# A table of steps for every piece of a chunk, fp8 transposes in the FFN, and a searched order for the end, in a two-layer scan, attention and FFN kernel

## The chip, the cores and the metric

The kernel runs on one core of one Trainium2 chip. Its engines work side by side, each through its own list of instructions in order: TensorE (PE, matmuls and transposes), VectorE (DVE), ScalarE (ACT), GpSimd (POOL) and SyncE (SP, which issues most DMAs). The metric is the device time of one execution in microseconds (us).

## What is computed

The input x is 4 images of 64 x 64 tokens with 96 channels, so 4 batches of 4096 tokens. Layer 0 adds to x a gated linear scan over the tokens of each batch, and layer 1 adds an attention without softmax and then an FFN whose numbers are rounded to fp8 (5 exponent and 2 mantissa bits) and fp16. Cut to what matters:

```python
# layer 0, of x after a group norm, per batch; S = 16 states per channel
proj = layernorm(x) @ W_in            # value, gate, delta (96 each), A, B, C (1536 each)
h_new = d * (A_t * h) + d * (B_t * u_t)      # along the tokens
y = sigmoid(gate) * sum_s(C_t * h_new)
x = x + y @ W_out
# layer 1
q, k, v = split(layernorm(x) @ Wqkv)          # 6 heads
y = (q @ k.T * D ** -0.5) @ v                 # no softmax
x = x + y @ Wff
h = relu(qlinear(layernorm(x), W1, b1))       # q_mul: fp8, q_acc: fp16
x = x + qlinear(h, W2, b2)
```

The attention has no softmax, so it is a matrix per batch: the kernel sums the gram matrix of the normalised tokens over a whole batch, and makes of it one 97 x 96 matrix (`rmat`) by which layer 1 multiplies each token. So layer 1 of a batch can't start before layer 0 of the whole batch has ended.

## The kernel before

**Chunks and steps.** A batch is cut into 8 chunks of 512 tokens, 32 chunks in all. A chunk's scan has 1536 rows (96 channels x 16 states), which are 12 tiles of 128 rows: one tile is one *step*, and there are K = 384 steps. The main loop at the end of the kernel goes through the steps and issues for each the same core work, in this order:

- PE: `b_proj` for the tile three steps on, `a_proj` for the next tile, `c_proj` for this one (three matmuls of 512 columns each);
- ACT: `b_copy` after `b_proj`, `keep` of the last column of h;
- POOL: `b_mul` for the tile two steps on, and, for the tiles whose number mod 12 is in `ON_POOL`, `c_mul_pool` of the tile before;
- DVE: `scan` of this tile (line 767), `a_mul` of the next (line 760), and for tiles not in `ON_POOL` `c_mul` (line 791);
- then `call(s)`: everything that the table `steps` holds for this step; last, `c_copy` on ACT for a tile in `ON_POOL`.

**Pieces of a chunk.** All else is put into `steps` by `at(step, fn)`, relative to the chunk's first step s0. The *front* (lines 696 to 718) makes the chunk's inputs: `load_x`, then `centre` and `scale` (POOL), `stats` (DVE), `rstd` (POOL), `apply` (ACT), `transpose` (PE, into the tile xnt), `affine` and `upper` (ACT), `low` (DVE, then three DMAs), the projections d and u (PE) with `d_out` (ACT) and `du_out` (DVE), `write` and `read` (DMAs which spread d and d*u over 128 partitions through DRAM into `rep`), and the gate. The *gathers* add up the four groups of states by DMA. The *tail* (lines 831 to 921) follows on the scan: `state_sum` (PE, tile y_ps), `gated` (DVE), `project_out` (PE, tile o_ps), `residual` and `stats` (DVE), `rstd` (POOL), `apply` (ACT), `transpose` (PE), `keep`, `spill` (DMA to DRAM), `gram` (PE) and its sum. `ffn` (lines 967 to 1106) is layer 1 of a chunk, 8 chunks later: `fetch` (DMA), `attention` (PE, tile a_ps), `residual`, `stats`, `rstd`, `apply` (ACT), `transpose` (PE, tile xq_ps), `quant_in` (ACT), three `hidden` matmuls (PE, tile h_ps) each with a `relu` of three ACT operations, `project_out` (PE), `round_out` (ACT), `bias_out` and `total` (POOL), `store` (DMA). `group_norm` computes the next batch's group norm.

**PSUM.** The core work has banks of its own (A twice, B, C, D); everything in `steps` takes its bank from one ring M of three, in the order in which it is issued, and so waits until the last reader of the tile three before is done.

**The end.** What would fall behind step 384 isn't put into `steps` but becomes a job of the list scheduler `Plan` (lines 387 to 460), with an engine, a cost, its predecessors and the buffers it takes and frees. `Plan.run` takes again and again the job that can start first; among those within `LOOK` us of it the one of lower rank, then the one with the longest chain behind it. In the end `apply` of layer 1 of batch 3 is on DVE (`apply_vector`), `relu` is on DVE, and `round_out` is on DVE for odd chunks. The first steps are ordered by the same class (`planned_start`).

The numbers that place the pieces before are:

```python
FRONT = -22
SUMS = -28
FFN0 = 28
ON_POOL = (1, 3, 6, 10)
```

Of the kernel before, what the change touches and what calls it, by code (L numbers as in the profile page):

```python
# [37 lines left out]
FRONT = -22  # L38
SUMS = -28
FFN0 = 28  # L40
ON_POOL = (1, 3, 6, 10)
# [4 lines left out]
def conv_attn_hybrid_kernel(  # L46
# [35 lines left out]
        "xn2": 1, "xq": 1, "h16": 1, "hr": 1, "hq": 1, "y16": 1, "yb": 1, "o": 1,  # L82
# [106 lines left out]
    xa_t, xal_t = [], []  # L189
    for r in range(2):  # L190
        t = const.tile([P, J, CA], F32, tag=f"xa{r}", name=f"xa{r}")
        nc.gpsimd.memset(t[:, :, C:CA], 1.0)
        xa_t.append(t)
        t = const.tile([CA, J, P], F32, tag=f"xal{r}", name=f"xal{r}")
        nc.gpsimd.memset(t[C:CA], 1.0)
        xal_t.append(t)

# [12 lines left out]
    w2_sb = sb("xn2", [C, HID], F32, "w2_sb")  # L210
# [125 lines left out]
    class LayerNorm:  # L336
# [32 lines left out]
        def apply(self, dst, src):  # L369
            for j in range(J):  # L370
                nc.scalar.activation(
                    dst[:, j, 0:C], src[:, j, :], AF.Identity,
                    bias=self.nmr[:, j : j + 1], scale=self.r[:, j : j + 1],
                )

        def apply_vector(self, dst, src):
            for j in range(J):
                nc.vector.tensor_scalar(  # L378
                    dst[:, j, 0:C], src[:, j, :], self.mv[:, j, 0:1], self.r[:, j : j + 1],
                    ALU.subtract, ALU.mult,  # L380
                )
# [5 lines left out]
    class Plan:  # L387
        HOP = 0.15
        LOOK = 0.3

# [19 lines left out]
        def run(self, fill=None):  # L410
# [13 lines left out]
            taken, back = self.taken, {}  # L424
            todo = list(self.jobs)
            while todo:
                best = None
                for n, j in enumerate(todo):
                    if any(a["end"] is None for a in j["after"]):
                        continue  # L430
                    t = self.time.get(j["engine"], 0.0)
                    for a in j["after"]:
                        hop = 0.0 if a["engine"] == j["engine"] else self.HOP
                        t = max(t, a["end"] + a["late"] + hop)
                    full = False
                    for b in j["take"]:
                        r = b.split(":")[0]
                        if len(taken[r]) >= self.rings[r]:
                            k = taken[r][-self.rings[r]]
                            full = full or k not in back  # L440
                            t = max(t, back.get(k, 0.0) + self.HOP)
                    if full:
                        continue
                    key = (t, j["rank"], -tail(j), n)
                    if best is None or t < best[0][0] - self.LOOK or (
                        t < best[0][0] + self.LOOK and key[1:] < best[0][1:]
                    ):
                        best = key, j
                (t, _, _, n), j = best
                todo.pop(n)  # L450
# [5 lines left out]
                j["end"] = self.time[e] = t + j["cost"]  # L456
                for b in j["take"]:
                    taken[b.split(":")[0]].append(b)
                for b in j["free"]:
                    back[b] = j["end"] + j["late"]  # L460
# [103 lines left out]
    def group_norm(b, s0):  # L564
# [11 lines left out]
        when = [s0 + SUMS + NT * n for n in range(NCH)]  # L576
# [119 lines left out]
    def front(b, i, s0, f=None):  # L696
        s = s0 + FRONT
        if f is None:
            f = Front(b, i)
            if (b, i) not in xt:  # L700
                at(s - 3, load_x, b, i)
            at(s, f.centre, nc.gpsimd)
            at(s + 1, f.scale, nc.gpsimd)
            at(s + 2, f.stats)
            at(s + 3, f.ln.rstd)
            at(s + 5, f.apply)
            at(s + 7, f.transpose)
            at(s + 8, f.affine)
            at(s + 9, f.upper)
            at(s + 9, f.low)  # L710
            at(s + 12, f.proj, 2)
            at(s + 13, f.d_out)
            at(s + 13, f.proj, 0)
            at(s + 14, f.du_out)
            at(s + 14, f.write)
            at(s + 15, f.read)
        at(s + 20, f.proj, 1)
        at(s + 21, f.gate_out)
# [89 lines left out]
    def state_sum(g, last=None, first=None):  # L808
# [17 lines left out]
        {"A": 2, "B": 1, "C": 1, "M": 3, "xal": 2, "xat": 1, "bu": 5, "h": 3, "rep": 2,  # L826
# [3 lines left out]
    end.last = {}  # L830

    def tail(b, i, s0):


        nm, g = f"{b}_{i}", b * NCH + i
        v, ln = {}, LayerNorm(1e-5, f"a_{nm}")
# [46 lines left out]
        def gram_add():  # L883
            nc.gpsimd.tensor_tensor(grams[b], grams[b], v["add"], ALU.add)

        plan = [
            (5, state_sum, g), (6, gated), (7, project_out), (8, residual), (8, ln.stats, t),
            (9, ln.rstd), (12, ln.apply, xa, t), (14, transpose), (15, keep), (16, spill),
            (21, gram), (22, gram_out),
        ]  # L890
        if i:
            plan.append((23, gram_add))
        for n, fn, *args in plan:
            if s0 + n < K:
                at(s0 + n, fn, *args)
        if s0 + plan[-1][0] < K:
            return
# [3 lines left out]
        job, a = end.job, None  # L901
        if s0 == K:
            for sh, late in ((0, 0.0), (2, 0.0), (3, 2.4)):
                w = job(f"wait{sh}", late, lambda: None)
                a = job("PE", 0.5, state_sum, g, sh, sh > 0, after=[a, w],
                        take=["B:y"] if sh == 0 else [])
            a = job("DVE", 0.7, gated, after=[a], free=["B:y"])
            a = job("PE", 0.5, project_out, after=[a], take=["B:o"])
            a = job("DVE", 0.56, residual, after=[a], free=["B:o"])
            a = job("DVE", 1.1, ln.stats, t, after=[a], take=[f"mv:a{i}"])  # L910
            a = job("POOL", 1.3, ln.rstd, False, after=[a])
        else:
            job("wait", 0.0, lambda: None, take=[f"mv:a{i}"])
        if s0 == K:
            applied = job("DVE", 1.3, ln.apply_vector, xa, t, after=[a], free=[f"mv:a{i}"])
        else:
            applied = job("ACT", 1.55, ln.apply, xa, t, free=[f"mv:a{i}"])
        a = job("PE", 0.4, gram, after=[applied, end.last.get("gram")], take=[f"B:g{i}"])
        end.last["gram"] = job("DVE", 0.25, gram_sum, after=[a], free=[f"B:g{i}"])
        a = job("PE", 0.45, transpose, after=[applied], take=[f"C:a{i}"])  # L920
        a = job("ACT", 0.57, keep, after=[a], free=[f"C:a{i}"], take=[f"xat:{i}"])
        end.last[b, i] = job("SP", 0.5, spill, after=[a], late=2.5, free=[f"xat:{i}"])
# [4 lines left out]
    def attn_matrix(b, s0):  # L927
# [31 lines left out]
        for n, (args, out) in enumerate(chain):  # L959
            if s0 < K:  # L960
                at(s0 + 24 + n, mm, *args)
                at(s0 + 24 + n, out)
            else:
                a = end.job("PE", 0.3, mm, *args, after=[a], take=[f"B:r{n}"])
                a = end.last["r"] = end.job("DVE", 0.25, out, after=[a], free=[f"B:r{n}"])

    def ffn(b, i, s0):
# [6 lines left out]

        def fetch():
            v["xa"] = xal_t[i % 2]
# [12 lines left out]
        def apply():  # L989
            v["xn"] = tile_of("xn2", "bu", [P, J, C], F32, "xn2")  # L990
            (ln.apply_vector if b == B - 1 else ln.apply)(v["xn"], t)

        def transpose():
            ps = v["ps"] = bank("C" if phase["end"] else "M", [C, TC], f"xq_ps_{nm}")
            for j in range(J):
                nc.tensor.transpose(ps[:, j * P : (j + 1) * P], v["xn"][:, j, :], ident)
# [365 lines left out]
```

## Time and profile before

| what | value |
|---|---|
| median of 3 runs | 1214.04 us (1212.67 to 1214.79) |
| the profiled execution | 1214.51 us, span 1212.8 us |
| granted clock of TensorE | 0.989 |
| first scan starts, last scan starts | 30.8 us, 1134.4 us |
| chunks 1 to 9 (layer 0 only), from scan to scan | 299.3 us, 33.3 us each |
| chunks 10 to 30 (with layer 1), from scan to scan | 733.1 us, 34.9 us each |
| rmat of batch 3 is there | 1150.5 us |
| `scan` on DVE | 336 of 1269 ns and 48 of 1210 ns |
| `b_mul` on POOL | 384 of 1496 ns |

The profile's page gives busy time for each engine, first as totals and then in slices. Durations in it overlap on one engine (an operation's end[...] lies behind the start of the next one), so what an operation costs an engine is read from the distance of two starts in the timeline. The list of waits says which engine stood idle, for which instruction, and who released it.

### The profile page before, as it was taken

The page shows a single profiled execution, that of the slowest core. Times are in us where ns is not written, and L with a number is a line of the kernel's source. Part 1 is how long each engine was busy: PE and PEld are TensorE (multiplying, and loading weights), DVE is VectorE, ACT ScalarE, POOL GpSimd, SP SyncE. Part 2 cuts the span into 40 slices and gives each one's busy share as a digit, 9 for nine tenths or more (in the row PEclk, how much of TensorE's full clock was granted, in tenths as well). Part 3 has the DMA queues.
Part 4 walks back from the last instruction along what each step waited for, and adds up shares of the span by engine and source line. Part 5 has one row for each costly group of instructions (what it writes and reads, how often), then busy time and mean ns, then how long its engine had stood idle before and what let it go on. Part 6 is the DMA issues. An engine that isn't in the chain of part 4 may idle for free. (4 is left out here: it accounts for less than half of the span.)

```text
span 1212.8 us, 19189 instructions
## 1 busy us (share of the span) xinstructions
PE 1155.5 (95%) x5888; PEld 872.8 (72%) x5888; DVE 1125.7 (93%) x2103; ACT 809.9 (67%) x1812; POOL 1031.6 (85%) x1171
## 2 busy tenths in 40 slices
PE   6899999999999999999999999999999999999884
PEld 5677777777777777777777777677777777777652
DVE  6799999999999999999999999999999999999794
ACT  4655656655565787777777777777777777776574
POOL 3988878888888888999999888999999899988654
PEclk8999999999999999999999999999999999999998
DMA  7656767677776676677667766766776667666221
GB/s 185 141 133 145 165 151 164 147 161 164 168 160 151 153 166 151 154 168 176 159 151 164 172 154 146 174 154 149 154 174 154 154 158 174 153 145 142 66 66 40
DMA packets 104289, 182.14 MB, mean 150 GB/s; under 512 B 42637, under 2 KB 50769, under 8 KB 104186
## 3 DMA queue, kind: packets, MB, share of 16 engines
q1 hardware_dynamic: 90060, 106.96, 36.5%
q0 software_dynamic: 13536, 73.93, 30.2%
q8 instruction: 47, 0.77, 0.3%
q14 instruction: 56, 0.46, 0.1%
q10 hardware_dynamic: 590, 0.02, 0.0%
HBM read 69.12 MB, written 24.77 MB: 77 GB/s over the span
## 5 line engine op out<-in xcount | busy, mean ns | idle before, releaser
L751 POOL TENSOR_TENSOR bu<-bu,rep 128x512 f32<-128x512 f32 x384 | 557.7, 1496 | 14.7 <-ACT bu L748 9.2
L748 ACT ACTIVATE bu<-Bps,b_bac 128x512 f32<-128x512 f32 x384 | 263.7, 687 | 286.0 <-PE Bps L244 269.0
L767 DVE TENSOR_TENSOR_SCAN h<-Aps,state,bu 128x512 f32<-128x512 f32 x336 | 426.4, 1269 | 13.2 <-POOL bu L751 3.5
L760 DVE SCALAR_TENSOR_TENSOR Aps<-Aps,b_bac,rep 128x512 f32<-128x512 f32 x384 | 282.5, 736 | 25.1 <-PE Aps L244 24.6
L244 PE MATMUL Bps<-xs,w 128*128 128x512 f32 x768 | 268.1, 430 | 3.7 <-ACT bu L748 3.4
L244 PE MATMUL Aps<-xs,w 128*128 128x512 f32 x768 | 249.6, 406 | 14.2 <-DVE h L767 13.3
L800 POOL TENSOR_TENSOR ch<-ch,h 128x512 f32<-128x512 f32 x128 | 193.5, 1512 | 2.6 <-ACT ch L797 2.4
L244 PEld LDWEIGHTS Aps<-xs,w 128*128 128x128 f32 x768 | 138.6, 189 | 70.5 <-DVE h L767 42.3
L244 PEld LDWEIGHTS Bps<-xs,w 128*128 128x128 f32 x768 | 129.4, 191 | 46.5 <-issue 24.3
L244 PE MATMUL Aps<-xl,w 128*128 128x512 f32 x384 | 152.6, 397 | 0.3 <-DMA w<-w 0.3
L244 PE MATMUL Bps<-xl,w 128*128 128x512 f32 x384 | 151.8, 395 | 0.0
L244 PE MATMUL Dps<-xs,w 128*128 128x512 f32 x384 | 121.1, 397 | 0.0
L244 PE MATMUL Cps<-xs,w 128*128 128x512 f32 x384 | 120.8, 395 | 0.0
L806 POOL DMA_DIRECT2D ch<-ch x94 | 89.0, 947 | 15.1 <-DMA ch<-ch 11.5
L791 DVE SCALAR_TENSOR_TENSOR ch<-Dps,b_bac,h 128x512 f32<-128x512 f32 x128 | 94.7, 740 | 0.5 <-PE Dps L244 0.4
L791 DVE SCALAR_TENSOR_TENSOR ch<-Cps,b_bac,h 128x512 f32<-128x512 f32 x128 | 95.0, 742 | 0.0
L244 PEld LDWEIGHTS Aps<-xl,w 128*128 128x128 f32 x384 | 72.4, 188 | 18.4 <-DMA w<-w 1.0
L244 PEld LDWEIGHTS Bps<-xl,w 128*128 128x128 f32 x384 | 72.5, 189 | 17.5
L244 PEld LDWEIGHTS Dps<-xs,w 128*128 128x128 f32 x384 | 72.4, 189 | 17.5
L244 PEld LDWEIGHTS Cps<-xs,w 128*128 128x128 f32 x384 | 72.3, 188 | 17.5
L244 PE MATMUL Dps<-xl,w 128*128 128x512 f32 x192 | 76.0, 396 | 0.0
L244 PE MATMUL Cps<-xl,w 128*128 128x512 f32 x192 | 75.7, 394 | 0.0
(196 smaller groups left out, 2056.0 us busy)
## 6 DMA issues: line engine op xcount, KB each, us to landing
ch<-ch POOLq DMA_DIRECT2D x94, 768.0 KB, 6.5
rep<-ddd SPq DMA_DIRECT2D x124, 384.0 KB, 6.4
ddd<-dd SPq DMA_DIRECT2D x31, 384.0 KB, 3.0
xl<-lo SPq DMA_DIRECT2D x62, 128.0 KB, 2.4
x<-in_x_dram SPq DMA_DIRECT2D x32, 192.0 KB, 2.9
xatd<-xat SPq DMA_DIRECT2D x32, 192.0 KB, 3.1
xal<-xatd SPq DMA_DIRECT2D x32, 192.0 KB, 5.8
out_dram<-o SPq DMA_DIRECT2D x32, 192.0 KB, 2.1
```

The lines of the kernel that those rows point to most:

```text
L244: nc.tensor.matmul(ps, lhsT=wt[:, n], rhs=mv, start=(n == 0), stop=(n == 2))
L748: nc.scalar.activation(self.bu, self.b_ps, AF.Identity, bias=self.bias(0))
L751: nc.gpsimd.tensor_tensor(self.bu, self.bu, rep[self.b, self.i][:, 1, self.cg], ALU.mult)
L760: nc.vector.scalar_tensor_tensor(self.a_ps, self.a_ps, self.bias(1), rep[self.b, self.i][:, 0, self.cg], ALU.add, ALU.mult,)
L767: nc.vector.tensor_tensor_scan(self.h, self.a_ps, self.bu, 0.0 if self.i == 0 else state[self.sh, self.cg], ALU.mult, ALU.add,)
L791: nc.vector.scalar_tensor_tensor(self.slot(), self.c_ps, self.bias(2), self.h, ALU.add, ALU.mult)
L800: nc.gpsimd.tensor_tensor(self.ch, self.ch, self.h, ALU.mult)
L806: nc.gpsimd.dma_start(chs[g, 0], chs.pop((g, sh)), accum_op=ALU.add)
```

## The change

1. The numbers for the pieces of front, gathers, tail and `ffn` become one table `AT` of steps relative to s0 (for `ffn` relative to the step 96 after its chunk's s0), with other values. x is loaded at -28 and centred at -15, 13 steps later, where it was loaded at -25 and centred at -22. `ON_POOL` is (1, 2, 7, 10).
2. In `ffn` the normalised tokens are written as fp8 into one of two constant tiles of 128 columns (`xn8`, zeros in the last 32), and the transposes are fp8 matmuls with an fp8 identity.
3. A group of pieces (such as `transpose`, `keep` and `spill`) either lies wholly before step 384, or wholly in the end (`place`). The jobs of the end follow from that: the tail of chunk 30 from `project_out` on, and the transposes of chunk 29.
4. `Plan.run` for the end makes 800 schedules with random additions to the ranks, and takes the one whose last job, by the costs of its own table, ends first. `planned_start` makes one, with `LOOK` 0.6 instead of 0.8.
5. In the end, `apply` of batch 3 is on DVE for even chunks and on ACT for odd ones, `round_out` the other way round, and `bias_out` and `total` of the last two chunks are on DVE.

```diff
-FRONT = -22
-SUMS = -28
-FFN0 = 28
-ON_POOL = (1, 3, 6, 10)
+AT = {
+    "load_x": -28, "centre": -15, "scale": -15, "stats": -14, "rstd": -14, "apply": -13,
+    "transpose": -12, "affine": -12, "upper": -11, "low": -11, "proj_d": -8, "d_out": -8,
+    "proj_u": -8, "du_out": -8, "write": -8, "read": -7, "proj_gate": 1, "gate_out": 2,
+    "gather1": 6, "gather2": 11, "gather3": 14,
+    "state_sum": 22, "gated": 23, "project_out": 24, "residual": 24, "stats_a": 26,
+    "rstd_a": 26, "apply_a": 28, "transpose_a": 31, "keep": 33, "spill": 40, "gram": 29,
+    "gram_out": 29, "gram_add": 33,
+    "fetch": 19, "attention": 26, "residual_f": 26, "stats_f": 27, "rstd_f": 27, "apply_f": 31,
+    "transpose_f": 34, "quant_in": 34, "hidden0": 37, "relu0": 39, "hidden1": 41, "relu1": 44,
+    "hidden2": 45, "relu2": 46, "project_f": 47, "round_out": 47, "bias_out": 47, "total": 48,
+    "store": 49,
+    "sums": -32,
+}
+ON_POOL = (1, 2, 7, 10)
...
+        t = const.tile([P, J, P], F8, tag=f"xn8{r}", name=f"xn8{r}")
+        nc.gpsimd.memset(t, 0.0)
...
+            rng = random.Random(1)
+            best = zero = [0.0] * len(self.jobs)
+            lates = schedule(zero, self.LOOK)
+            for n in range(self.tries):
+                wide = n < self.tries // 4
+                share, size = (1.0, rng.choice((0.5, 2.0, 5.0))) if wide else (0.02, 2.0)
+                bias = [
+                    b + rng.gauss(0.0, size) if rng.random() < share else b
+                    for b in (zero if wide else best)
+                ]
+                found = schedule(bias, rng.choice((0.05, 0.15, self.LOOK)))
+                if found and (lates is None or found[0] < lates[0]):
+                    lates, best = found, bias
...
-            at(s, f.centre, nc.gpsimd)
-            at(s + 1, f.scale, nc.gpsimd)
...
+        for name, fn, *args in plan:
+            at(s0 + AT[name], fn, *args)
...
+    def place(plan, s0):
+        done = set()
+        for group in plan:
+            if max(s0 + AT[name] for name, *_ in group) < K:
+                for name, fn, *args in group:
+                    at(s0 + AT[name], fn, *args)
+                    done.add(fn)
+        return done
...
-            (5, state_sum, g), (6, gated), (7, project_out), (8, residual), (8, ln.stats, t),
-            (9, ln.rstd), (12, ln.apply, xa, t), (14, transpose), (15, keep), (16, spill),
-            (21, gram), (22, gram_out),
...
+        vector = b == B - 1 and i % 2 == 0
...
-            v["xn"] = tile_of("xn2", "bu", [P, J, C], F32, "xn2")
-            (ln.apply_vector if b == B - 1 else ln.apply)(v["xn"], t)
+            v["xn"] = next_of(xn8_t, "xn8")
+            (ln.apply_vector if vector else ln.apply)(v["xn"], t, saturate=False)
...
-                nc.tensor.transpose(ps[:, j * P : (j + 1) * P], v["xn"][:, j, :], ident)
+                nc.tensor.matmul(
+                    ps[:, j * P : (j + 1) * P], lhsT=v["xn"][:, j, :], rhs=ident8,
+                    start=True, stop=True,
+                )
...
-            (0, attention), (1, residual), (1, ln.stats, t), (2, ln.rstd),
-            (5, apply), (7, transpose), (8, quant_in),
-            (9, hidden, 0), (10, relu, 0), (11, hidden, 1), (12, relu, 1),
-            (13, hidden, 2), (14, relu, 2), (15, project_out), (16, round_out),
-            (17, bias_out), (18, total), (19, store),
...
-        plan.LOOK = 0.8
+        plan.LOOK = 0.6
...
-            for n, sh in ((7, 1), (10, 2), (13, 3)):
+            for sh in range(1, NSH):
...
-                    at(s0 + n, gather, g, sh)
+                    at(s0 + AT[f"gather{sh}"], gather, g, sh)
```

In the old plans the tail's numbers count from the step 12 after s0 and those of `ffn` from the step 96 + 28 after it; in the new table the tail's count from s0, and those of `ffn` from s0 + 96.

## The prediction

> **What bounds the kernel now.** I read the page's busy times first, then busy time by stretches, then VectorE's waits, then two engine timelines.
>
> ```profile
> PE 1155.5 (95%) x5888; PEld 872.8 (72%) x5888; DVE 1125.7 (93%) x2103; ACT 809.9 (67%) x1812; POOL 1031.6 (85%) x1171
> 106.50:339.00 232.50, 228.50 (x1084) 172.89 (x1083) 224.89 (x376) 135.51 (x327) 198.97 (x214) 1.00 0.71 156
> 795.40:1002.60 207.20, 205.14 (x1054) 155.47 (x1053) 200.13 (x371) 149.34 (x331) 191.72 (x217) 1.00 0.72 159
> DVE Aps L760 <- PE Aps L244: 21.2, 34, 1.4
> DVE h L767 <- POOL bu L751: 3.5, 4, 0.9
> ```
>
> No engine is far from full. The second line is seven chunks of batch 0, without layer 1's FFN (33.2 us each, DVE idle 7.6/7 = 1.09); the third is six chunks with it (34.53 each, DVE idle 7.07/6 = 1.18). The last two lines (waits, 100 to 1100 us) say what DVE lacks: matrix A from PE, hardly ever POOL. The DVE timeline shows the place, and gives the durations by the starts that follow each other:
>
> ```profile
> 627.61 1.28 DVE L767 TENSOR_TENSOR_SCAN h<-Aps,state,bu 128x512 f32<-128x512 f32 x1
> 629.74 0.76 DVE L760 SCALAR_TENSOR_TENSOR Aps<-Aps,b_bac,rep 128x512 f32<-128x512 f32 x1 [0.85 <-PE Aps L244]
> 630.44 0.75 DVE L791 SCALAR_TENSOR_TENSOR ch<-Cps,b_bac,h 128x512 f32<-128x512 f32 x1
> 631.11 0.74 DVE L647 SCALAR_TENSOR_TENSOR dd<-dug_ps,b_dug,dd 96x512 f32<-96x512 f32 x1
> 631.76 0.72 DVE L346 BATCH_NORM_STATS2 st_c<-z 128x6 f32<-128x96 f32 x4
> ...
> 632.69 1.25 DVE L767 TENSOR_TENSOR_SCAN h<-Aps,state,bu 128x512 f32<-128x512 f32 x1
> 633.86 0.73 DVE L760 SCALAR_TENSOR_TENSOR Aps<-Aps,b_bac,rep 128x512 f32<-128x512 f32 x1
> 634.50 0.74 DVE L791 SCALAR_TENSOR_TENSOR ch<-Dps,b_bac,h 128x512 f32<-128x512 f32 x1
> 635.16 0.54 DVE L987 TENSOR_TENSOR x<-a_ps,x 128x384 f32<-128x384 f32 x1
> 635.74 0.74 DVE L346 BATCH_NORM_STATS2 st_f<-x 128x6 f32<-128x96 f32 x4
> ...
> 636.67 1.25 DVE L767 TENSOR_TENSOR_SCAN h<-Aps,state,bu 128x512 f32<-128x512 f32 x1
> 616.78 0.39 PE L244 MATMUL Dps<-xl,w 128*128 128x512 f32 x1
> 617.01 0.60 PE L996 MATMUL xq_ps<-ident,xn 128*96 128x128 f32 x4
> 617.36 0.71 PE L244 MATMUL Bps<-xs,w 128*128 128x512 f32 x2
> ```
>
> DVE: scan 1.17, a_mul 0.64, c_mul 0.66, a residual 0.58, one set of stats 0.93, du_out 0.65; gated 0.60 and low 0.59 likewise. PE: 0.232 a big matmul, so 2.09 for a step's nine and 0.70 for one of d, u, gate; by the same reading of starts, four fp32 transposes 0.43, o_ps 0.88, a_ps 0.81, gram 0.63, y_ps 0.99, the FFN's second matmuls y2 0.52, one hidden 0.23. POOL: b_mul and c_mul_pool 1.25, centre and scale 0.97, an rstd 1.8 to 1.9, a gather's issue 0.69, bias_out 1.0, total 0.89; with gram_add 0.35 that is 31.9 a chunk.
>
> **What the skill says.** "PSUM — Partial Sum Buffer", Engine vs sequencer instructions: ScalarE, VectorE and GpSimd are strict FIFO, and matmuls run in program order. The trace agrees: the a_mul at 629.74 holds all behind it. So a wait for a bank stops PE for everybody. "TensorE: Matmul & The Clock Gate", Back-to-back issue gap: 128 columns take 134 cycles, about 56 ns at 2.4 GHz; its weight-path section: plain fp8 has no gain over bf16. Here twelve fp8 matmuls of 96 columns (604.86 to 605.38) take 43 ns each, so 128 columns some 58; the fp32 transposes take 0.43 for four (610.99 to 611.42). "Perfetto Trace Analysis", Optimization Strategy: a gap that repeats can mean too few buffers. Here the gap repeats at one place of each chunk.
>
> **Method.** Call a step's place its number mod 12. I sum each place's DVE and PE work, and follow PE's lead: how long before DVE a step starts on PE. Next lead = lead + DVE's work − PE's. It can't exceed DVE's work after the scan of the step before + 0.70 (A needs the bank which that scan frees), and below 0.53 DVE waits (B and A take 1.4, the last matmul ends 0.3 later, a_mul comes at 1.17).
>
> Every step has scan and a_mul on DVE (1.81) and nine matmuls on PE (2.09). On top of it DVE has, before: c_mul but at 1, 3, 6, 10; du_out and the front's stats at 4; attention's residual and stats at 5; gated at 6; the tail's residual and stats at 8; low at 11. PE: h0 at 1; d and xat 2; u and h1 3; a_ps 4; y_ps and h2 5; o_ps and y2 7; gx 8; xnt and gram 9; gate 10; xq 11. After, DVE: c_mul but at 1, 2, 7, 10; residual 0; low 1; the tail's stats and attention's residual 2; its stats 3; du_out 4; the front's stats 10; gated 11. PE: xnt and o_ps 0; gate and h0 1; a_ps 2; d, u, gx 4; gram and h1 5; xat 7; h2 9; y_ps and xq 10; y2 11.
>
> Before, with layer 1, places 0 to 11: DVE 2.5 1.8 2.5 1.8 4.1 4.0 2.4 2.5 4.0 2.5 1.8 3.1; PE 2.1 2.3 3.2 3.0 2.9 3.3 2.1 3.5 2.5 3.2 2.8 2.5. DVE gets light steps (1 to 3) while PE has its d, u and transposes there; the lead falls from 1.6 to below the limit, and DVE waits 0.15 + 1.21 = 1.36 at places 3 and 4. Without layer 1: 0.92. Measured idle is 1.18 and 1.09, so the method holds within 0.2.
>
> **The change, part by part.** *Moves.* The same instructions, so no busy time is gained. After: DVE 3.0 2.4 3.3 3.4 3.1 2.5 2.5 1.8 2.5 2.5 2.7 3.1; PE 3.4 3.0 2.9 2.1 3.9 3.0 2.1 2.5 2.1 2.3 3.3 2.6. Stats no longer fall together with du_out or in one step with a residual and c_mul (4.0 was three times the load; now 3.4 is the largest), and places 3 and 4, where d and u are now both computed, follow a light PE step. Without layer 1 the lead stays between 0.6 and 2.0: no wait left, 0.92 gained, taken as 0.9.
>
> *A new wait.* Bank ring M has three buffers. At place 0 it goes to xnt and o_ps, at place 1 to gate, then to hidden0 (37), which so gets xnt's bank. Its last reader is low, the last DVE work of the same step (2.4 after its start; PE is there at 3.1 less its lead, some 2). PE stops 0.4 to 0.8, and behind it stand B and A of step 2, so DVE waits 0.86 there for a_mul. Total waits with layer 1 0.86 instead of 1.36: 0.5 gained.
>
> *fp8 transposes.* 0.43 − 0.23 = 0.2 of PE at place 10. The stop at place 1 resets the lead afterwards, so this only keeps it above the limit at place 11: worth 0 to 0.2 a chunk; I take it as contained in the 0.5. The written fp8 of apply on ACT: an fp8 write of 512 is 0.63 against 0.59 for fp16 (groups at L1015 and L1012), ACT is idle a third of the time: nothing. The ring of two xn8 frees SBUF and adds no wait. Memsets and one copy on POOL at the start: three instructions of about 0.5 (memsets of 512 columns at L188), between 0 and 1.5; I take 0.
>
> *Front made short.* centre and scale (0.97 each), stats, rstd (1.82), apply, transpose now lie within places 9 to 0. rstd waits for stats in its own step: POOL ends it 2.0 into place 11, ACT's apply (1.54) ends 0.4 into place 0, PE wants z at 0.5 to 0.7. It fits with 0.1 to 0.3, and another 0.2 until the residual of place 0 is late. POOL's load at places 2 and 3 is 5.1 + 4.4 against 6.7 of DVE, but b_mul is made two steps ahead: the one for place 6 still has 0.5. rep: in the trace its last part lands 11.9 after du_out; places 5 to 9 now last 11.8 (15.3 before), and b_mul wants it 0.6 later still. SP: low's DMAs stand ahead of store in place 1; spill now goes behind write in place 4 and before read, which waits 3.1 for write anyway. x is loaded 13 steps ahead instead of 3; a load lands in 2.9, so either way it is hidden. Buffers of x: 172 steps of life against 15 × 12. All this: 0.
>
> *The end.* From 1150.5, when batch 3's matrix is there:
>
> ```profile
> 1150.50:1204.50 54.00, 40.31 (x289) 27.38 (x287) 42.10 (x140) 37.75 (x58) 27.26 (x35) 0.94 0.20 56
> ```
>
> DVE 42 and ACT 38 of 54. Four of batch 3's applies go from DVE (14.0 for eight) to ACT (+6.2), and DVE takes the last two bias and total (+2.8): DVE 38, ACT 44. The larger sum grows by 2, so a gain can only come from the 12 us of idle that the random search removes; also 0.5 at the very end, where two POOL operations of 0.92 become DVE ones of some 0.6. The tail of chunk 30 from project_out on (DVE 1.5, PE 1.5, POOL 1.9) is now in the end, in gaps of 4.5 us that DVE has between 1137 and 1143. Bounds: +4 and −10. I take −4.
>
> *Start.* LOOK is 0.6 instead of 0.8, the order can differ: ±2, taken as 0.
>
> **Sum.** 9 chunks × 0.9 = 8.1, 21 × 0.5 = 10.5, end 4: 22.6. The profiled execution took 1214.5 (span 1212.8), the runs' median is 1214.0: 1192.
>
> **Rivals.** (1) *No stop at hidden0*, because low comes sooner than I think or the ring is not what binds: waits with layer 1 of 0.4 or less and a better end, 21 × 0.45 = 9.5 and 5 more: 1177. For it: low waits for nothing else; against: low is DVE's last in its step. (2) *The moves gain little with layer 1*: PE has 33.2 of work a chunk, DVE 33.4, POOL 31.9; three nearly full queues that wait for each other keep some 0.5 idle. Then only batch 0 gains: 1206. (3) *Slower: z too late.* POOL's rstd in place 10 falls behind (rep late, gather waiting, rstd behind stats); z comes late, PE stops at the transposes with o_ps behind them. From 0.45 late each us costs one in each of 30 chunks; from 1.2 late it eats the gain. At 1.8: 30 × 1.35 = 40 against 22: 1232. For it: POOL idles only 2 us a chunk; against: rep lands at 11.3 to 12.5 in all 30 chunks.
>
> **How the numbers follow.** 1192: 0.45; rival 1: 0.22; rival 2: 0.2; rival 3: 0.13. Its own range is 1184 to 1200; the 8 in 10 reach 1172 to 1214. A change of 0.2%, 2.4 us, is what can be told from none. Faster: 0.45 + 0.22 + most of rival 2 = 0.84; same 0.03; slower 0.13.
>
> **What would show it.** Right: DVE's wait for A gone from places 3 and 4 and there at place 2; PE waiting at h_ps for lo; chunks of 34.0 with layer 1 and 32.3 without; xq_ps near 0.06 a matmul. Wrong: PE waits at xnt_ps for z, DVE at scan for bu, or chunks above 34.5.

## The result, and the profile after

The changed kernel is slower by 0.9%: 1224.69 us median of four runs (1221.91 to 1227.67) beside 1213.96 for the kernel before, a ratio of 1.009 [1.0064, 1.0115]. The forecast was 1192. The profiled execution took 1221.9 us, span 1220.2.

In which stretch the time went is read from the starts of the scans:

| stretch, us | before | after | difference |
|---|---|---|---|
| start to first scan, and chunk 0 | 30.8 + 41.8 | 29.9 + 42.2 | −0.5 |
| chunks 1 to 9, without layer 1 | 299.3 | 310.1 | +10.8 |
| chunks 10 to 20 | 386.6 | 388.6 | +2.0 |
| chunks 21 to 30 | 346.5 | 343.1 | −3.4 |
| chunk 31, to its last scan | 29.5 | 29.7 | +0.2 |
| last scan to the span's end | 78.4 | 76.6 | −1.8 |

The page's totals after:

```profile
PE 1166.2 (96%) x5885; PEld 878.7 (72%) x5885; DVE 1120.6 (92%) x2091; ACT 816.5 (67%) x1828; POOL 1030.3 (84%) x1178
```

and one of the stretches (start and end, length, busy time of PE, PEld, DVE, ACT and POOL with instructions, then the clock, the DMA engines' mean busy share and GB/s):

```profile
106.50:339.00 232.50, 223.75 (x1039) 169.29 (x1040) 216.97 (x357) 133.49 (x316) 194.59 (x208) 0.99 0.68 150
```

The counts of instructions hardly changed (PE 5885 after, 5888 before; DVE 2091 and 2103). PE's busy time rose by 10.7 us all the same: 4.1 of that lie behind the last scan, and a busy PE can also be one that is held up within an instruction (the four transposes at 315.60 below last 1.39 us, and 0.60 where nothing holds them). In this stretch DVE is idle 15.5 us (7.6 before) and got through 357 instructions instead of 376. So the loss is waiting, and the waits between 100 and 1100 us say for what (four engines: who waits for which instruction of whom, us in total, times, longest):

```profile
DVE x L920 <- PE o_ps L915: 20.8, 24, 2.4
DVE Aps L817 <- PE Aps L269: 14.8, 38, 1.3
...
POOL bu L808 <- DMA rep<-ddd: 33.4, 12, 6.6
...
PEld xnt_ps L681 <- ACT z L396: 26.7, 59, 3.3
...
ACT z L396 <- POOL nmr_c L384: 61.4, 29, 4.9
```

Read from the bottom up, this is one chain. ACT waits 29 times for POOL's rstd; PE waits for ACT's `z`; and DVE waits for `o_ps`, which stands behind the transposes of `z` on PE. At its head POOL waits for `rep`, the front's d and d*u, which comes by DMA. In the same window before, none of the first three is among the large waits. DVE's wait for A went down from 21.2 to 14.8, so the rearrangement did what it was to do, and lost more elsewhere. (ACT stands idle for 24.8 us at that place in a kernel below that is faster, so its 61.4 us alone wouldn't prove a loss; PE's and DVE's waits do.)

One chunk of it, in POOL's timeline (start, duration, line, out<-in; in brackets the idle time before it):

```profile
299.91 0.94 POOL L863 DMA_DIRECT2D ch<-ch  x1
...
308.49 0.40 POOL L954 TENSOR_TENSOR gram<-gram,gadd 97x97 f32<-97x97 f32 x1
311.92 1.29 POOL L808 TENSOR_TENSOR bu<-bu,rep 128x512 f32<-128x512 f32 x1 [3.03 <-issue]
313.18 0.23 POOL L378 TENSOR_SCALAR rstd_c<-mv_c 128x4 f32<-128x4 f32 x1
...
314.85 0.20 POOL L384 TENSOR_TENSOR nmr_c<-nmr_c,rstd_c 128x4 f32<-128x4 f32 x1
```

and in the timelines of ACT, PE and DVE:

```profile
315.08 1.54 ACT L396 ACTIVATE z<-z,nmr_c,rstd_c 128x96 f32<-128x96 f32 x4 [2.61 <-POOL nmr_c L384]
...
315.60 1.39 PE L681 MATMUL xnt_ps<-ident,z 128*96 128x128 f32 x4 [0.35 <-ACT z L396]
316.83 1.05 PE L915 MATMUL o_ps<-w_o,yg 97*128 97x96 f32 x8
...
317.92 0.56 DVE L920 TENSOR_TENSOR x<-o_ps,x 128x384 f32<-128x384 f32 x1 [0.72 <-PE o_ps L915]
```

POOL stands still from 308.9 to 311.9. The timeline can't name the cause ("issue"), but the last of the 64 completions of the four `rep` DMAs is at 311.71, 0.2 before the b_mul starts. The b_mul is the next chunk's first; rstd stands behind it, though its input was there at 311.70. ACT, PE and DVE follow.

Why `rep` is late is seen on SP's queue, which issues it, beside POOL's gather (at 299.91 in POOL's timeline above):

```profile
295.65 0.33 SPq L744 DMA_DIRECT2D ddd<-dd  x1
...
298.79 1.75 SPq L751 DMA_DIRECT2D rep<-ddd  x4
300.59 0.44 SPq L125 DMA_DIRECT2D x<-in_x_dram  x1
301.13 0.45 SPq L130 DMA_DIRECT2D gx<-in_x_dram  x1
```

`read` is four DMAs of 384 KB, issued from 298.79 on. POOL's first gather, 768 KB, is issued 1.1 us after the first of them, and x and gx follow. At the same chunk before, the gather came 3.4 us after:

```profile
290.05 1.76 SPq L688 DMA_DIRECT2D rep<-ddd  x4
293.49 0.91 POOL L806 DMA_DIRECT2D ch<-ch  x1
```

For chunks 2 to 31 `rep`'s last completion comes a median of 15.6 us after du_out's end (12.3 to 17.4); before, 12.5 (12.2 to 13.1). The b_mul that uses it starts a median of 0.2 us behind that completion; before, 3.3 us. Two things moved together: the gather from step 7 to step 6, towards `read` in place 5, and the loads of x and gx, which SP issued behind `low`'s DMAs and now, since their steps have nothing to wait for, issues right behind `read`. The experiments take them apart.

### The profile page after: what moved, and what is told of

Read it like the earlier page. It is cut to its first block, busy times and chain, and to the rows that moved or that the text cites. A ratio compares the mean times of both kernels' runs of the same rounds, so it can differ in the third digit from the quotient of the medians.

```text
span 1220.2 us, 19141 instructions
## 1 busy us (share of the span) xinstructions
PE 1166.2 (96%) x5885; PEld 878.7 (72%) x5885; DVE 1120.6 (92%) x2091; ACT 816.5 (67%) x1828; POOL 1030.3 (84%) x1178
## 5 line engine op out<-in xcount | busy, mean ns | idle before, releaser
L808 POOL TENSOR_TENSOR bu<-bu,rep 128x512 f32<-128x512 f32 x384 | 512.6, 1383 | 90.2 <-DMA rep<-ddd 38.4
L269 PE MATMUL Aps<-xs,w 128*128 128x512 f32 x768 | 243.3, 398 | 3.3 <-DVE h L824 2.9
L857 POOL TENSOR_TENSOR ch<-ch,h 128x512 f32<-128x512 f32 x128 | 174.2, 1361 | 10.1 <-ACT ch L854 9.7
L269 PEld LDWEIGHTS Aps<-xs,w 128*128 128x128 f32 x768 | 143.2, 188 | 42.5 <-DVE h L824 9.2
L396 ACT ACTIVATE z<-z,nmr_c,rstd_c 128x96 f32<-128x96 f32 x124 | 47.9, 457 | 63.1 <-POOL nmr_c L384 63.1
L269 PE MATMUL Cps<-xl,w 128*128 128x512 f32 x192 | 75.9, 395 | 0.0
```

The source lines that it names most:

```text
L269: nc.tensor.matmul(ps, lhsT=wt[:, n], rhs=mv, start=(n == 0), stop=(n == 2))
L396: nc.scalar.activation(dst[:, j, 0:C], src[:, j, :], AF.Identity, bias=self.nmr[:, j : j + 1], scale=self.r[:, j : j + 1], **kw,)
L808: nc.gpsimd.tensor_tensor(self.bu, self.bu, rep[self.b, self.i][:, 1, self.cg], ALU.mult)
L857: nc.gpsimd.tensor_tensor(self.ch, self.ch, self.h, ALU.mult)
```

## The experiments

Steps are as in `AT`; where not said otherwise a kernel is the changed one with that one edit. Each was timed in one of four groups, on four chips, beside the kernel before, and "ratio" is against that; the medians of the kernel before in these groups lie within 1.2 us of each other. Stretches and landings are those of each kernel's one profiled execution.

**Which half of the change costs.** `old_table`: all values of `AT` and `ON_POOL` are those of the kernel before; fp8 transposes, the searched end and `planned_start` stay.

```diff
-    "load_x": -28, "centre": -15, "scale": -15, ...
+    "load_x": -25, "centre": -22, "scale": -21, ...
-ON_POOL = (1, 2, 7, 10)
+ON_POOL = (1, 3, 6, 10)
```

> The changed kernel with the steps and ON_POOL of the kernel before in its table; the fp8 transposes, the rule for the end and its search, and LOOK 0.6 stay. Theory (the table is what costs, through rep that lands late): the layer-0 chunks 1 to 9 come back to 299 us, rep lands 12.5 us after du_out and POOL waits for it hardly at all; with the end 2 us shorter and 0.1 to 0.2 us a chunk from fp8 transposes the run takes 1207 to 1212 us. Rival (the rest costs: fp8 transposes, fp8 write or the new end): it stays at 1220 us or above.

1208.56 us (1205.12 to 1210.51), ratio 0.9952 [0.9939, 0.9964]. Chunks 1 to 30 take 1032.7 us in its trace (1032.4 before), and the end 71.4 (78.4 before). So the rest of the change gains 5.5 us, in the end, and the loss is the table's. Two sizes were missed: the end gained 7.0 us where 2 were expected, and with the old steps the fp8 transposes gain nothing (chunks 10 to 30 take 733.0, and 733.1 before).

**Gather or loads.** Both kernels change the order of transfers, one that of SP's loads, one that of POOL's gather; the third does both.

```diff
# loads_behind_low
-    "load_x": -28,   "fetch": 19,
+    "load_x": -23,   "fetch": 13,
-                at(max(when[n] - 7, when[n - 1]), load_gx, b, n)
+                at(max(when[n] - 3, when[n - 1]), load_gx, b, n)
# gather_late
-    "gather1": 6,
+    "gather1": 8,
# both: all of these
```

> The changed kernel, but load_x (-28 to -23), fetch (19 to 13) and the load for the group norm (3 steps ahead instead of 7) all at place 1, behind low's three DMAs, so that none of the three goes out right behind read. Theory (these loads and gather1 share the DMA engines with read and delay rep): rep lands 13 to 14 us after du_out instead of 15.6, b_mul of the next chunk starts 1 to 2 us sooner, DVE's waits for o_ps at place 0 mostly go; 1195 to 1208 us. Rival (POOL is late through its heaped work at places 9 to 3, rep is incidental): rep lands sooner but rstd, z and the transposes stay where they are; 1220 us or above.

> The changed kernel with gather1 at step 8 instead of 6; the three loads stay behind read. Theory: gather1 (768 KB) is the other transfer beside read; moved 2 steps (4.5 us) on it takes less from read, rep lands about 14.5 us after du_out, a third of the loss goes: 1214 to 1220 us. If gather1 is the main rival of read: 1205. If it has nothing to do with it, or pushes POOL's gather2 on: 1224 or above.

> Both moves at once: the loads at place 1 and gather1 at step 8. Theory: nothing lies beside read, rep lands 12.5 us after du_out as before the change; z is on time, DVE's wait at place 0 is gone; then the wait for hidden0's bank at place 1 can show. 1190 to 1203 us. Rival (POOL's heaped work): no more than 5 us better than the changed kernel, 1219 or above.

| kernel | median, us | ratio | rep after du_out | chunks 1–9 / 10–30 | end |
|---|---|---|---|---|---|
| loads_behind_low | 1232.11 (1227.47 to 1242.98) | 1.0161 [1.0126, 1.0196] | 15.1 | 318.1 / 741.1 | 75.0 |
| gather_late | 1194.98 (1192.51 to 1197.95) | 0.9834 [0.9821, 0.9847] | 12.5 | 296.7 / 718.0 | 78.7 |
| both | 1210.21 (1206.36 to 1211.9) | 0.9962 [0.995, 0.9974] | 12.55 | 304.0 / 725.5 | 75.5 |

Moving the one gather by two steps gives 29.7 us, where I expected a third of the loss, and brings `rep` back to 12.5. The loads were a miss of mine: with the gather at 6, `rep` stays late without them behind `read`, and the loads moved make things worse, because gx, three steps ahead, comes too late for its transposes (PE waited for gx's load 17.2 us in 6 waits, up to 5.9). `late_x_behind_low` takes gx out of that:

```diff
-    "load_x": -28,   "fetch": 19,   "gather1": 6,
+    "load_x": -23,   "fetch": 13,   "gather1": 8,
```

> gather_late with load_x at -23 and fetch at 13 (SP issues both behind low's DMAs, as in the kernel before), gx's load left where it is. Theory (rep already lands at 12.5 us, so the x and xal loads beside read cost nothing more; what hurt the kernel named both was gx): 1193 to 1198 us. Rival (SP's order matters by itself: loads behind low are late for centre and attention): 1200 us or more.

1194.13 us (1192.39 to 1195.74), ratio 0.9835 [0.9819, 0.9851]: as gather_late. With the gather out of the way, x and xal may stand on either side. It differs from `both` in gx's load alone, so that load is what costs `both` its 16 us.

In gather_late POOL is no longer held. `read`, then POOL's timeline at the same chunk, where rstd waits for nothing but its own input:

```profile
289.20 1.75 SPq L751 DMA_DIRECT2D rep<-ddd  x4
...
295.38 0.93 POOL L863 DMA_DIRECT2D ch<-ch  x1
...
300.01 1.28 POOL L808 TENSOR_TENSOR bu<-bu,rep 128x512 f32<-128x512 f32 x1
302.01 0.23 POOL L378 TENSOR_SCALAR rstd_c<-mv_c 128x4 f32<-128x4 f32 x1 [0.72 <-DVE mv_c L373]
```

and PE's, which passes from C to the transposes without a gap:

```profile
305.07 0.40 PE L269 MATMUL Cps<-xl,w 128*128 128x512 f32 x1
305.31 0.60 PE L681 MATMUL xnt_ps<-ident,z 128*96 128x128 f32 x4
305.74 1.03 PE L915 MATMUL o_ps<-w_o,yg 97*128 97x96 f32 x8
```

**Bytes, or POOL's queue.** The gather is also an instruction of POOL, ahead of a product; so it could be the place in POOL's queue that counts. `gather_at_7` moves it half as far, `gather_at_9` a step farther. `gather_eighth` leaves it at 6 but adds only 64 of 512 columns; the other columns of the second state group are missing from the sum. The packets in the trace show that it has not as many descriptors as before, but three times as many: 384 of 256 bytes, where the whole gather has 128 of 6144.

```diff
# gather_at_7 and gather_at_9
-    "gather1": 6,
+    "gather1": 7,      # and 9
# gather_eighth
-        nc.gpsimd.dma_start(chs[g, 0], chs.pop((g, sh)), accum_op=ALU.add)
+        t = chs.pop((g, sh))
+        m = TC // 8 if sh == 1 else TC
+        nc.gpsimd.dma_start(chs[g, 0][:, :, 0:m], t[:, :, 0:m], accum_op=ALU.add)
```

> gather1 goes from step 6 to 7, halfway to the kernel gather_late (step 8, 1195.0 us, rep lands 12.5 us after du_out's end). Theory (what delays rep is the overlap of the gather's transfer with read's): one step is some 2.5 to 3 us of 5.6 us of overlap taken away, so rep lands at 13.5 to 14.5, and since b_mul has about 1 us between, the time is 1198 to 1208 us. Rival (POOL's issue of the gather at place 6, ahead of the product of place 7, is what costs): place 7 has a product of POOL too, so nothing is gained until 8: 1220 or more.

> gather1 stays at step 6 with as many descriptors, but adds only the first 64 of 512 columns, 96 KB instead of 768 KB; the other columns of the second state group are left out of the sum. Theory (bytes in flight beside read delay rep): rep lands at 12.5 to 13 us and the time is at or a little under that of gather_late, 1190 to 1197 us. Rival (the number of descriptors, or POOL's place in its queue): rep lands near 15 and the time is 1215 or more.

> gather_late with gather1 at step 9. Theory (at 8 it is already clear of read in most chunks, and gather2 at 11 follows it): rep lands at 12.4 us, the few chunks that still lose at 8 (4 and 5, 36.0 and 34.2 us) gain 1 to 3 us in all: 1191 to 1196 us. Rival (the three gathers queue behind each other, state_sum at 22 becomes late): 1200 us or more, with waits of TensorE for ch at y_ps.

gather_at_7: 1208.27 us (1202.78 to 1211.02), ratio 0.9937 [0.9918, 0.9956]. gather_eighth: 1192.7 (1191.77 to 1196.09), 0.9821 [0.9809, 0.9834], `rep` at 12.8. gather_at_9: 1194.33 (1192.1 to 1195.66), 0.9835 [0.9819, 0.9851], without the gain that I expected in chunks 4 and 5. An eighth of the bytes at the same place in POOL's queue gives all that moving it gives, with three times the packets and a longer issue on POOL (1.33 us, 0.91 for the whole gather). So neither POOL's queue nor the number of packets costs; it is the bytes, or the size of the packets, which this run changed with them. But the dose is not what I expected: at 7 `rep` doesn't land a little later everywhere, it lands at a median of 12.7 with 5 chunks beyond 14. Laid over each other, the 150 chunks of the kernel before, the changed one and the gathers at 7, 8 and 9 show a step. The first column is how long after the first of `read`'s four issues the gather is issued, the others how long from that first issue to `rep`'s last completion, in us:

| gather issued after | chunks | shortest | median | longest |
|---|---|---|---|---|
| under 1.0 | 11 | 12.1 | 12.9 | 14.3 |
| 1.0 to 1.5 | 10 | 11.8 | 12.7 | 13.5 |
| 1.5 to 2.0 | 12 | 9.1 | 10.9 | 12.8 |
| 2.0 to 3.0 | 22 | 9.1 | 9.4 | 10.1 |
| over 3.0 | 95 | 8.9 | 9.3 | 11.7 |

`read`'s four issues take 1.75 us of SP. A gather issued before they are through mostly costs some 3 us, one issued later next to nothing. In the changed kernel 22 of 30 gathers come under 1.75, at 7 it is 7 of 30, at 8, 9 and before none. The step number alone doesn't say it: the kernel before has its gather at 7 too, but no less than 3.4 us behind `read`'s first issue.

The DMA packets in these traces show what lies behind the step. Issued under 1.5 us, the gather moves its first packet a median of 5.8 us after `read`'s first issue, and in the median chunk all its 128 packets are done before `read` lands. Issued 2 us after it or later, its first packet comes at 9.2, and in the median chunk none is done before `read` lands. So `read` waits for the whole gather or for nearly none of it: 768 KB at the 209 GB/s of the stretch below are 3.8 us, by estimate, and `read` loses some 3.4. `gather_eighth`'s packets go out among `read`'s too (first at 5.8, 97% done), and `read` takes 9.6. That the order of issue decides which goes first fits all of this; it is inferred, as no run varied the order alone.

The stretch from `read`'s issue to its landing shows why there is no room (columns as in the stretches above; the last but one is the DMA engines' busy share). In the kernel after:

```profile
298.80:311.70 12.90, 12.90 (x59) 9.53 (x60) 12.04 (x22) 5.29 (x8) 9.55 (x9) 1.00 0.94 209
```

In gather_late:

```profile
289.20:298.30 9.10, 9.10 (x43) 7.34 (x42) 8.24 (x10) 3.92 (x6) 7.75 (x7) 1.00 0.93 190
```

`read` nearly fills the 16 engines by itself: in the last line some 1.6 of the 1.7 MB moved are its own. The Trainium skill says in "DMA: Bandwidth & Descriptors", Issuing engines are not separate DMA queues, that DMAs of the scalar, sync and gpsimd engines run on the same 16 DMA engines and interleave. The longer stretch at nearly the same share (0.94 and 0.93) agrees on the engines; that they interleave is so here for a gather issued early, while one issued 2 us later mostly ran behind `read`.

**What fp8 and the search are worth.** Both start from gather_late. `late_fp32` writes the tokens as fp32 and transposes them as before; `late_unsearched` takes the list schedule without the random ones.

```diff
# late_fp32
-        t = const.tile([P, J, P], F8, tag=f"xn8{r}", name=f"xn8{r}")
+        t = const.tile([P, J, C], F32, tag=f"xn8{r}", name=f"xn8{r}")
...
-                nc.tensor.matmul(
-                    ps[:, j * P : (j + 1) * P], lhsT=v["xn"][:, j, :], rhs=ident8, ...
+                nc.tensor.transpose(ps[0:C, j * P : (j + 1) * P], v["xn"][:, j, :], ident)
# late_unsearched
-    end.tries = 800
+    end.tries = 0
```

> gather_late with the FFN's normalised tokens written as fp32 into two tiles of 96 columns and transposed as fp32, as in the kernel before. Theory of the prediction (0.43 against 0.23 us of TensorE at place 10, worth 0 to 0.2 us a chunk in 22 chunks): 1195 to 1200 us. Rival (TensorE's lead decides at place 10 and 11, so each 0.2 us is paid in full and once more in the end): 1201 us or more.

> gather_late with tries = 0: the end's list schedule as the rule makes it, without the 800 random ones. Theory of the prediction (the search is what the end gains): the part from the last scan's start to the span's end grows from 78.7 us by 2 to 8, so 1197 to 1203 us. Rival (the schedule's own costs are too far from the chip for the search to be worth anything): 1193 to 1197 us, no difference to be measured.

late_fp32: 1198.19 us (1197.9 to 1199.35), ratio 0.9865 [0.9852, 0.9878]. Its chunks 10 to 30 take 722.1 us instead of 718.0, so fp8 saves 0.2 each, which is what PE saves by the distance of two starts: four transposes take 0.33 in fp8 (712.59 to 712.92 in gather_late) and 0.53 in fp32 (715.73 to 716.26 in late_fp32). late_unsearched: 1202.62 us (1196.88 to 1204.72), ratio 0.9891 [0.9874, 0.9908]; the search is worth 7.6 us by the medians, with runs that overlap those of gather_late. The end is 83.2 us, at a mean clock of 0.85; at the same clock the searched order took 76.3 and 77.3 (gather_at_9 and gather_at_7), so 6 to 7 less.

**The chunks that stay long, and the end.** In gather_late chunks 21 to 30 take a median of 33.4 us, near PE's 33.2 of work, but chunks 12 to 20 some 35. They have the next batch's group-norm transposes, `gx_ps`, at place 4 beside d and u. `late_sums_8` and `late_sums_6` move them to place 8 and to place 6. `late_tail_in_time` gives chunks 29 and 30 steps before 384 for the parts of their tails that the table pushed into the end.

```diff
# late_sums_8 and late_sums_6
-    "sums": -32,
+    "sums": -28,      # and -30
# late_tail_in_time
-        done = place(plan, s0)
+        early = {
+            N - 3: {"spill": 35},
+            N - 2: {"state_sum": 18, "gated": 19, "project_out": 20, "residual": 20,
+                    "stats_a": 21, "rstd_a": 22},
+        }
+        done = place(plan, s0, {**AT, **early.get(g, {})})
```

> gather_late with the next batch's group-norm transposes (gx_ps, fp32, about 0.35 us of TensorE) at -28, place 8, in place of -32, place 4. In gather_late the chunks that have them (5 to 20) take 34.7 to 35.4 us where those without (21 to 30) take 33.4, and place 6 is 3.2 us long instead of 2.5. Theory (TensorE's lead: place 4 has d, u and gx, 4.2 us of TensorE against 3.1 of VectorE, and the lead is spent at place 6, whereas place 8 has only 2.1): chunks 12 to 20 fall to 33.6 to 34.1, so 15 chunks by about 0.9 us: 1179 to 1185 us. Rival (what costs is the group norm's load and its ScalarE work, wherever they stand): 1192 us or more.

> gather_late with the group-norm transposes at -30, place 6. At place 8 they made chunks 10 to 20 some 2.5 us longer while chunks 5 to 9, without layer 1, grew 0.9 us shorter; at place 8 ScalarE has relu1 of the FFN, which chunks 5 to 9 lack. Theory (two limits at once: TensorE's lead at place 4, ScalarE's queue at place 8; place 6 is light on both, TensorE 2.1 us and ScalarE nothing but the core's copies): chunks 5 to 8 at 31.7, chunks 12 to 20 at 33.6 to 34.2, 1179 to 1186 us. Rival (gx costs the same wherever it stands once the FFN is there): 1192 us or more.

> gather_late in which the tail of chunk 30 up to its rstd and the transposes and spill of chunk 29 stand at steps before 384 again (state_sum 18 to rstd 22, spill 35), so that the end no longer has them. Theory (the table's later steps push work behind the last scan, which is why the end takes 78.7 us here and 71.4 with the steps of before): the part from the last scan's start shrinks by 1 to 4 us and the scans before it grow by at most 1: 1191 to 1194 us. Rival (these jobs lie in idle time of the end): 1194 to 1197 us.

late_sums_8: 1213.83 us (1207.57 to 1217.41), ratio 0.9992 [0.9977, 1.0007], far from what I expected. Chunks 6 and 7, without layer 1, fell to 31.7 as they should, but chunks 10 to 20 rose from 382.4 to 403.9 us. The loss is on ACT, an engine that the argument had left out. ACT's timeline at such a place:

```profile
574.24 0.65 ACT L572 ACTIVATE gx_ps<-gx_ps,gmc 96x512 f32<-96x512 f32 x1 [1.17 <-PE gx_ps L543]
...
575.04 0.57 ACT L572 ACTIVATE gx_ps<-gx_ps 96x512 f32<-96x512 f32 x1
...
575.63 0.57 ACT L1104 CAST h<-h_ps 128x512 f16<-128x512 f32 x1
...
577.52 0.67 ACT L805 ACTIVATE bu<-Bps,b_bac 128x512 f32<-128x512 f32 x1
```

and PE's:

```profile
576.08 0.39 PE L1096 MATMUL h_ps<-xq,w_q 96*128 96x512 fp8e5 x1
578.24 0.73 PE L269 MATMUL Bps<-xs,w 128*128 128x512 f32 x2 [1.77 <-ACT bu L805]
```

At place 8 ACT first waits 1.17 for the transposes, then has gx's two passes and relu1's three operations, and only then the copy of B, for whose bank PE waits 1.77. From 100 to 1100 us PE's waits for that copy come to 18.3 us (3.2 in gather_late), most of the 21.5 lost. Chunks without layer 1 have no relu1. late_sums_6, at a place where ACT is light too: 1186.92 us (1186.37 to 1188.42), ratio 0.9773 [0.9757, 0.9789], the best here and just above the 1179 to 1186 expected. In the traces 5.4 us of the gain over gather_late lie in chunks 1 to 30; the end, 3.8 shorter, has the same order (on that see the last section). Chunks 6 and 7 take 31.6; chunks 10 to 20 take 379.9, only 2.5 less in all, where I expected 9 or so. Chunks 12 to 20 keep 34.8 while chunks 21 to 30 take 33.5. PE is idle for under 0.2 us in either, and the transposes themselves take it 0.35; the rest stays open.

late_tail_in_time: 1194.29 us (1193.52 to 1196.69), ratio 0.9835 [0.9822, 0.9849]: no difference from gather_late. The end is 76.8 us, but the last chunk's scans take 30.8 instead of 28.7.

## Why the prediction was wrong

**The step that failed** is in "Front made short": "rep: in the trace its last part lands 11.9 after du_out; places 5 to 9 now last 11.8 (15.3 before), and b_mul wants it 0.6 later still", summed up as "All this: 0". The time of a transfer was carried over as a constant into a kernel in which other transfers stand beside it. The table in the change shows gather1 going from 7 to 6, which brings it from two steps behind `read` to one, and the prediction never priced that move. In place of 11.9 the runs show 15.6 (12.5 with gather1 at 8, which alone gives back 29.7 us). The 11.9 was also misread: it is the first completion of the last `read`, and the last one comes at 12.5. The first completion wouldn't even have shown the delay: it comes at 12.0 in the changed kernel. By the prediction's own sum that takes the whole margin of 11.8 + 0.6 − 11.9 = 0.5 us. The sum was a little too strict there: in gather_late, with `rep` at 12.5, the b_mul starts a median of 1.0 us later. The words on SP ("x is loaded 13 steps ahead ... either way it is hidden") did come out harmless, but not for the reason given: a load of x issued behind `read` lands in a median of 11.6 us (8.2 in gather_late), not 2.9, and has 13 steps of time.

With gather1 at 8, a step that changes no work, the kernel takes 1195 us against the forecast's 1192. That it comes so near is luck in part: the parts below miss in both directions. Read against gather_late:

- *The rival that came true.* "Slower: z too late" is what happened, link by link (rep late, rstd behind, PE stopped at the transposes with o_ps behind them), and its trigger was named. So were its signs: PE waits at `xnt_ps` for z, and chunks with layer 1 take 34.8 us. What spoke against it was that `rep` landed by 12.5 us in all 30 chunks (12.2 to 13.1 by last completions); but that held for before's distance between read and gather. Its price was 40 us; measured from the first scan to the last it is 1113.8 after against 1087.1 in gather_late, 26.7.
- *Moves, without layer 1.* Forecast 8.1 for chunks 1 to 9, measured 2.6. Chunks 1 to 3 gained 5.7 in all, but chunks 4 and 5 lost 3.2, where one batch's group norm ends and the next one's begins; with `sums` at place 6 it is 5.3. The forecast counted gx in place 4, with 3.9 of PE's work, and found no wait there; moving it away gained 2.7. Chunk 4 takes 36.0 with `sums` at 4, 6 or 8 (34.2 before); why is open.
- *Moves, with layer 1.* Forecast 0.5 a chunk, 10.5; measured 733.1 − 718.0 = 15.1, of which 4.1 are the fp8 transposes (late_fp32). The other 11.0 agree with the forecast, but by luck: it had a new wait that isn't there, and no wait at gx.
- *The new wait at hidden0* isn't there: 0 instead of 0.86. In all 20 chunks between 440 and 1100 us `hidden0` starts 0.23 or 0.24 after the gate's last matmul, which is the usual distance. DVE's waits for A from 820 to 1088 us, eight chunks, are 2.6 us:

```profile
DVE Aps L817 <- PE Aps L269: 2.6, 9, 0.4
```

  PE is busy for 166.96 of 167.00 us from 787 on. So it runs behind, not ahead, and that it has no lead to lose at hidden0 is the likely reason; no run tried it alone. Rival 1, that this stop isn't there, had the mechanism, though its 1177 was too good.
- *fp8 transposes.* Forecast 0 to 0.2 a chunk, measured 0.2: the upper bound, as is to be expected where PE sets the pace. One of them takes 0.08 us by the starts, not 0.06, and the fp32 ones were 0.1 dearer for four as well, so the difference was right.
- *The end.* Forecast −4 with bounds of +4 and −10. Measured 74.8 to 79.1 with this order against 78.4, at mean clocks of 0.79 to 0.91 in the end against 0.91; the four at 0.90 or 0.91 (late_sums_6, loads_behind_low, both, late_x_behind_low) took 74.8 to 75.9, so 2.5 to 3.6 less. The size was right. The search alone measured more than that (6 to 7.6). That the jobs which the table adds behind the last scan take part of it back is likely, not shown: with the steps of before the end is 71.4 at 0.90, but `late_tail_in_time` gained nothing by moving such jobs forward.

## What to carry over

When a DMA is moved, price what it flies beside. Here the DMA engines were 0.93 to 0.94 busy between `read`'s issue and its landing, a transfer issued among its parts delayed it by about its own bytes, and the landing time read from the old trace no longer held. Take a transfer's landing from its last completion, and keep the slack of its consumer as a number, since a table that shortens the way from producer to consumer spends exactly that slack. And before work goes into a light place of one engine's list, add up the same place on every engine that handles its result.

## What the hardware showed

- A gather of 768 KB issued less than 1.5 us after the first of four reads lengthens them from 9.3 to about 12.8 us; issued 2 us after it or later it mostly costs them nothing. The step lies near where the last of the four has been issued (1.75 us). In the first case the gather's packets are done before the reads land; in the second they start at a median of 9.2 us, when the reads are nearly over. Issued early, the gather takes a median of 11.3 us (7.9 to 13.2) from issue to landing; the other two gathers of a chunk take about 6.
- The same order of instructions behind the last scan took 74.8 us in one execution and 79.1 in another, and these two differ in the granted clock. The records show only 1.0 and 0.5; the figure of a stretch is a mean. Half speed was granted for 14.5 us of the end in the first and for 33.8 in the second. From the last scan's start to the span's end in late_sums_6:

```profile
1111.50:1186.30 74.80, 53.05 (x412) 36.97 (x410) 49.67 (x181) 51.57 (x91) 39.51 (x59) 0.90 0.22 62
```

  and in gather_eighth:

```profile
1115.30:1194.40 79.10, 62.63 (x412) 43.36 (x410) 50.01 (x181) 51.46 (x91) 39.23 (x59) 0.79 0.21 58
```

  PE's 412 instructions took 53.1 us at a clock of 0.90 and 62.6 at 0.79, while DVE and ACT took the same. Clock and length don't go together in every run: gather_late's end took 78.7 at 0.88, the changed kernel's 76.6 at 0.83. A gain of 2 us in this end can't be told from one profile.
